# Two places in a queue: GpSimd's word ahead of a fold, and an addition moved across a block boundary

## The chip, the cores and the metric

The kernel runs on one core of a Trainium2 chip. The metric is the device time of one execution in microseconds; the median of three runs stands for the kernel. The engines have short names in the profile: PE is TensorE (matrix products; PEld its weight loads), DVE is VectorE, ACT is ScalarE, POOL is GpSimd, SP is SyncE, which only issues DMAs. Each engine takes its own instructions strictly in the order in which the program lists them; engines wait for each other through semaphores.

## The reference

Two layers run one after the other on `x` of shape (16, 256, 32, 32) in float32. Each layer normalises its input in groups (`_gn`; the 16 groups are pairs of neighbouring columns of the last axis), forms q, k and v with three 256 x 256 matrices, and lets four heads of width 64 attend over all 1024 positions. The result is added to the layer's input:

```python
q = proj(Wq, bq); k = proj(Wk, bk); v = proj(Wv, bv)
sim = jnp.einsum('bhdi,bhdj->bhij', q, k)
rel = (rel_h + rel_w).reshape(heads, d, n)
qpos = jnp.einsum('hdi,bhdj->bhij', rel, q)
attn = jax.nn.softmax(sim + qpos, axis=-1)
out = jnp.einsum('bhdn,bhmn->bhdm', v, attn)
x = x + out            # once for each layer
```

## The kernel before

**Blocks.** A *unit* `u` is one image in one layer, 32 of them. A unit has two pairs of heads (`pr`), and each pair two halves of 512 query positions (`half`). Such a half is a *block*, numbered `n` from 0 to 127; `b` = `n` mod 4 is its place in the unit, so `half` is 0 in even blocks and 1 in odd ones. `block(n)` (L619) lists the work of a block for all engines. The order is written by hand, and nothing reorders it.

**One block.** The 1024 key positions are cut into eight tiles `j`. For each, VectorE writes the position terms into a PSUM tile (`seed`, L344, product on L349), TensorE adds the product of k and q (`scores`, L373, product on L385), and ScalarE writes the exponential to a tile `p` (L394). TensorE then multiplies v with the eight tiles `p` (`attend`, L409, product on L419). Scores 0 of the next block are put between the two halves of `attend`; scores 1 to 3 come at the beginning of the block, the others further on, and between them stand two *pieces* of later work: projections to q, k or v (`project`, `values`) or the position terms (`positions`, L314). `prepare` (L593) names the pieces: in b = 1 they are a k projection and positions, in b = 3 a v projection and positions. The sums over a group for the normalisation of later units (`norm_sums`, `norm_squares`, `norm_mean`, `norm_var`) and the normalisation itself (`norm_apply`) lie on ScalarE, with two small products on TensorE and `rstd` on GpSimd (L237).

**The word.** A piece or an `attend` is done in two stretches, which write the same PSUM banks from different rows of TensorE. The second stretch may only start when the first has ended. `stretches` (L157) sees to it through GpSimd: `word` (L164) is a one-element memset (`token`, L166) on GpSimd that waits for the last product of the first stretch, and the second stretch waits for the memset. So a word stands in GpSimd's queue and goes out only after all that stands before it. Where `word` isn't called, the second stretch calls it itself.

**The denominators.** The softmax needs the sum over all keys. `add_up(blk, j)` (L397, instructions on L403 and L405) lets VectorE add tile `p` number `j` into `acc`. Additions 1 to 4 stand inside the block, addition 5 near its end, addition 6 at the beginning of the next block. Everything further is done by DMAs that accumulate, which GpSimd issues: `add_last` (L435) adds the eighth tile, `fold` (L438) adds rows 64 to 127 of `acc` to rows 0 to 63. From there on SP copies 32 rows to a *stack* that gathers the two blocks of a pair (`stack_up`, L449), GpSimd adds the other 32 rows to it (`fold_again`, L457), and `fold_stack` (L462) halves the stack's 128 rows five times (D = 64, R = 32, R/2, R/4, R/8 rows). `spread_sums` (L467) takes the four rows left to where `reciprocals` (L508) reads them in an even block; `finish` (L541) multiplies and adds the residual in an odd block.

**GpSimd's queue in an odd block** is, in order: fold D of the pair before, `add_last` of the block before, the first piece's word, fold R, `fold`, fold R/2, the `attend` word, fold R/4, `fold_again` (two DMAs), fold R/8, and in b = 3 the two instructions for `rstd`. In an even block it is: `add_last`, two words, `fold`, the `attend` word, `fold_again`. **VectorE's queue at the end of an odd block** is: addition 5, `finish`, the mean or variance out of PSUM, seeds 1 to 3 of the next block, and then in the even block addition 6, seed 4, addition 1.

The last two blocks have no pieces and are written separately (`block_without_pieces`, L756).

Of the kernel before, what the change touches and what calls it, by code (L numbers as in the profile page):

```python
# [52 lines left out]
def fast_path(ctx, tc, sh, x, layers, out, W, den_all, token, good, flag):  # L53
# [27 lines left out]
    B, C, H, N, CC, NT, NH, D, GT = (  # L81
        sh.B, sh.C, sh.H, sh.N, sh.CC, sh.NT, sh.NH, sh.D, sh.GT
    )
# [313 lines left out]
    def add_up(blk, j):  # L397
        u, pr, half = blk
        if j == 0:
            return  # L400
        if j == 1:
            accs[blk] = apool.tile([P, 2, HALF], F32, tag="acc", name=f"acc_{u}_{pr}_{half}")
            nc.vector.tensor_tensor(accs[blk], probs[blk, 0], probs[blk, 1], ALU.add)  # L403
        else:
            nc.vector.tensor_tensor(accs[blk], accs[blk], probs[blk, j], ALU.add)  # L405
# [26 lines left out]
    R = P // 4  # L432
# [29 lines left out]
    def fold_stack(u, pr, rows_):  # L462

        stack = stacks[u, pr]
        nc.gpsimd.dma_start(stack[:rows_], stack[rows_ : 2 * rows_], accum_op=ALU.add)  # L465
# [116 lines left out]
    blocks = [(u, pr, half) for u in range(NU) for pr in range(CC) for half in range(NH)]  # L582
# [36 lines left out]
    def block(n):  # L619
        blk = blocks[n]  # L620
        u, b = divmod(n, BPU)
        pr_, half = blk[1:]

        stacked = blocks[n - 3][:2] if half == 1 and n > 2 else None
        summed = blocks[n - 4][:2] if half == 0 and n > 3 else None
        before = blocks[n - 5][:2] if half == 1 and n > 4 else None
        after = blocks[n + 1] if n + 1 < len(blocks) else None
        previous = blocks[n - 1] if n > 0 else None
        one, two = u + 1 < NU, u + 2 < NU

        pieces = u + 1 < NU or b < 2
        if u + 1 == NU and b == 1:
            widen(u, 1)
        f0, f1, f2, f3 = ring
        folded = n - 1 < FOLDED
        if not pieces:
            return block_without_pieces(n, half)

        if stacked:
            fold_stack(*stacked, D)  # L640
        if previous:
            add_up(previous, 6)
            if folded:
                add_last(previous)
            else:
                add_up(previous, 7)
        for j in range(1, 4):
            scores(blk, j)
        (first, first_out), (second, second_out) = prepare(u, b)
        first(0)  # L650
        if b == 0 and one:
            norm_apply(u + 1, range(0, 1))
        if b == 1 and two:
            norm_sums(u + 2, range(9, 11))
        seed(blk, 4, f1)
        scores(blk, 4)
        add_up(blk, 1)
        if b == 0 and one:
            norm_apply(u + 1, range(1, 5))
        if b == 1 and two:  # L660
            norm_sums(u + 2, range(11, 12))
        if b == 2 and two:
            norm_squares(u + 2, range(0, 5))
        second(0)
        if half == 1:
            second_out()
        first.word()
        if half == 0:
            second.word()
        if stacked:  # L670
            fold_stack(*stacked, R)
        if previous and folded:
            fold(previous)
        if stacked:
            fold_stack(*stacked, R // 2)
        first(1)
        first_out()
        seed(blk, 5, f0)
        scores(blk, 5)
        if previous and folded:  # L680
            stack_up(previous)
        add_up(blk, 2)
        if half == 0:
            second(1)
            second_out()
        seed(blk, 6, f1)
        scores(blk, 6)
        if half == 0:
            ring[2:] = f3, f2
        seed(blk, 7, ring[2])  # L690
        scores(blk, 7)
        add_up(blk, 3)
        add_up(blk, 4)

        if after:
            seed(after, 0, f0)
        if summed:
            reciprocals(*summed)
        if n in check:
            next(checks)  # L700
        if b == 0 and one:
            norm_apply(u + 1, range(5, 9))
        if b == 0 and two:
            norm_sums(u + 2, range(0, 2))
        if b == 1 and two:
            norm_sums(u + 2, range(12, G))
        if b == 1 and one:
            norm_apply(u + 1, range(9, 11))
        if b == 2 and two:
            norm_squares(u + 2, range(5, 11))  # L710
        po = psum2(ring[3], f"po_{n}")
        values_of_p = attend(blk, po)
        values_of_p(0)
        if two and half == 1:
            if b == 1:
                mean_out = norm_mean(u + 2, filled(f1, f"pm_{n}", 0.0))
            else:
                mean_out = norm_var(u + 2, filled(f1, f"pm_{n}", EPS / 2))
        if after:
            scores(after, 0)  # L720
        values_of_p.word()
        if stacked:
            fold_stack(*stacked, R // 4)
        if previous and folded:
            fold_again(previous)
        if stacked:
            fold_stack(*stacked, R // 8)
            spread_sums(*stacked)
        if half == 1 and u + 3 < NU and units[u + 3][1] == 0 and u > 0 or n == 3:
            load_x(units[u + 3][0], range(pr_, pr_ + 1) if u > 0 else range(CC))  # L730
        add_up(blk, 5)
        if before:
            finish(*before)
        if two and half == 1:
            mean_out()
        if after:
            for j in range(1, 4):
                seed(after, j, ring[j % 3])
        if b == 0 and two:
            norm_sums(u + 2, range(2, 9))  # L740
        if b == 1 and one:
            norm_apply(u + 1, range(11, G))
        if b == 2 and two:
            norm_squares(u + 2, range(11, G))
        values_of_p(1)
        take_out(blk, po)
        pos[n] = po
# [8 lines left out]
    def block_without_pieces(n, half):  # L756

        blk = blocks[n]
        u, pr, _ = blk
        f0, f1, f2, f3 = ring  # L760
        summed = blocks[n - 2][:2] if half == 0 else (u, pr)
        before = blocks[n - 4][:2] if half == 0 else blocks[n - 3][:2]
        first = index[summed + (0,)]
        if half == 0:
            add_up(blocks[n - 1], 6)
        add_up(blocks[n - 1], 7)
        for j in range(1, 4):
            scores(blk, j)
        sums_of_p(blocks[first:n], pos[n - 1])
        keep_sums(pos[n - 1], first, n - first)  # L770
        if half == 1:
            finish(*before)
        else:
            reciprocals(*before)
        add_up(blk, 1)
        seed(blk, 7, f2)
        add_up(blk, 2)
        add_up(blk, 3)
        for j, tag in ((4, f1), (5, f0), (6, f1)):
            scores(blk, j, tag)  # L780
        reciprocals(*summed, n - first)
        scores(blk, 7)
        add_up(blk, 4)
        if half == 0:
            seed(blocks[n + 1], 0, f0)
        po = pos[n] = psum2(f3, f"po_{n}")
        values_of_p = attend(blk, po)
        values_of_p(0)
        if half == 0:
            finish(*before)  # L790
            scores(blocks[n + 1], 0)
        if half == 0:
            seed(blocks[n + 1], 1, f1)
            seed(blocks[n + 1], 2, f2)
        add_up(blk, 5)
        if half == 0:
            seed(blocks[n + 1], 3, f0)
        add_up(blk, 6)
        if half == 0:
            values_of_p(1)  # L800
            take_out(blk, po)
            return
        add_up(blk, 7)
        acc = accs.pop(blk)
        pd = psum2(f0, "pd")
        sums_on_rows(acc, pd)
        values_of_p(1)
        finish_half(u, pr, 0, outs[u, pr][:, 0, :], rdens[u, pr][:, :HALF])
        rden = rdens[u, pr][:, HALF:]
        nc.vector.reciprocal(rden, pd[:, 0, :])  # L810
        pd = psum2(f2, "pd_columns")[:, 0, : 2 * HALF // P]
        sums_on_columns(acc, pd)
        finish_half(u, pr, 1, po[:, :, :QUART], rden)
        list(in_range(flatden[:, 8 * checked : 8 * n], 1))
        list(in_range(pd, 2))
        nc.vector.tensor_reduce(good[:, 3:4], good[:, 0:3], AX.X, ALU.min)
        pc = psum2(f1, "pc")[0:1, 0, 0:1]
        nc.tensor.matmul(pc, good[:, 3:4], W.ones[:, 0:1], start=True, stop=True)
        nc.vector.tensor_copy(flag, pc)
# [404 lines left out]
```

## Time and profile before

| what | value |
|---|---|
| median of three runs | 2554.23 us (2549.47 to 2559.25) |
| the profiled execution | 2554.61 us |
| its span | 2552.8 us |
| granted TensorE clock, mean over the span | 0.998 |
| `token` memsets (L166) | 320 |
| folds of the stack (L465) | 310, 62 of each size |
| additions after the first of a block (L405) | 644, 1214 ns each |

A row of the list of waits gives the engine, what it was about to do, what ended its waiting, then the total in us, the number of times and the longest. A row of the timeline gives the start, the duration in us, the engine, the line and the tiles (what is written, an arrow, what is read), the number of instructions drawn together, and in brackets the idle time before with what ended it. The end of a matmul is modelled and reaches past the start of the next group; the step from one group to the next is therefore read from starts. A row of the DMA issues gives the queue, the count, the size and the median time from issue to landing.

### The profile page before, as it was taken

Reading aid. Unit: us, or ns where it says so; the run is one execution under the profiler, and the core shown is the slowest. Engines: PE = TensorE matmul, PEld = TensorE weight load, DVE = VectorE, ACT = ScalarE, POOL = GpSimd, SP = SyncE. Lnnn points to the kernel's source line nnn. Section 1 sums busy time; section 2 is a strip of 40 time slices with the busy share of each in tenths; the row PEclk is TensorE's granted clock in tenths of the full one; section 3 lists DMA queues with packets and bytes.
Section 4 is the critical chain, followed back from the end, with each engine's and each line's share of the span. In section 5 each row is a group of like instructions: output and inputs, shape, how many; then the busy total and the mean of one; then the engine's idle time right before and its main releaser. Section 6 shows DMA issues by size and latency. Waiting matters only on the chain.

```text
span 2552.8 us, 86089 instructions
## 1 busy us (share of the span) xinstructions
PE 2520.5 (99%) x37474; PEld 1330.9 (52%) x37474; DVE 2263.9 (89%) x2135; ACT 1950.1 (76%) x3874; POOL 836.6 (33%) x1194
## 2 busy tenths in 40 slices
PE   8999999999999999999999999999999999999997
PEld 4555555554555555555555555555555555555554
DVE  6888989988989899898899898988988999989997
ACT  6778777787777877777877778777778777787753
POOL 1333333323333233333333332333323333323320
PEclk9999999999999999999999999999999999999999
DMA  3343444454444444444444444444444444344441
GB/s 90 71 79 74 82 90 77 79 107 95 86 91 95 95 82 81 97 86 89 97 88 87 91 90 83 84 95 98 86 95 99 87 79 91 70 83 79 87 92 58
DMA packets 119537, 221.05 MB, mean 87 GB/s; under 512 B 53736, under 2 KB 55272, under 8 KB 119152
## 3 DMA queue, kind: packets, MB, share of 16 engines
q0 software_dynamic: 53568, 129.58, 30.5%
q1 hardware_dynamic: 65584, 85.90, 12.1%
q8 instruction: 295, 4.83, 0.8%
q14 instruction: 90, 0.74, 0.1%
HBM read 51.78 MB, written 17.30 MB: 27 GB/s over the span
## 4 chain that ended last, share of the span: by engine, by line
PE 88%; DMA 3%; DVE 2%; POOL 1%; issue 1%; SPq 0%; ACT 0%; POOLq 0%; DVEq 0%; ACTq 0%
PE po L419 31%; PE ps L385 31%; PE pk L268 8%; PE pv L298 8%; PE pq L268 8%; PE pa L326 2%; DMA acc<-p 1%; DMA stack<-acc 1%; DVE acc L405 1%; DVE ps L349 1%; POOL rstd L237 1%; DMA acc<-acc 0%; POOL stack L460 0%; POOL stack L465 0%; POOL acc L436 0%
## 5 line engine op out<-in xcount | busy, mean ns | idle before, releaser
L349 DVE TENSOR_TENSOR ps<-abt 128x1024 f32<-128x1024 f32 x1018 | 1227.4, 1229 | 255.2 <-ACT p L394 155.1
L394 ACT ACTIVATE p<-ps,shift 128x1024 f32<-128x1024 f32 x1024 | 1092.5, 1115 | 328.7 <-PE ps L385 325.7
L385 PE MATMUL ps<-q,k 64*64 64x512 f32 x8192 | 990.2, 591 | 0.9 <-DVE ps L349 0.9
L419 PE MATMUL po<-p,v 64*64 64x256 f32 x16384 | 930.5, 376 | 0.0
L419 PEld LDWEIGHTS po<-p,v 64*64 64x64 f32 x16384 | 628.7, 133 | 364.7 <-issue 77.7
L405 DVE TENSOR_TENSOR acc<-acc,p 128x1024 f32<-128x1024 f32 x644 | 781.6, 1214 | 4.9
L385 PEld LDWEIGHTS ps<-q,k 64*64 64x64 f32 x8192 | 303.3, 133 | 406.5 <-issue 222.8
L465 POOL DMA_DIRECT2D stack<-stack x310 | 266.7, 860 | 372.8 <-DMA stack<-acc 155.3
L166 POOL MEMSET token<- 1x1 f32 x320 | 44.8, 140 | 853.9 <-PE po L419 426.9
L268 PE MATMUL pk<-xn,Wk 64*64 64x512 f32 x2048 | 244.4, 593 | 7.0 <-POOL token L166 7.0
L460 POOL DMA_DIRECT2D stack<-acc x248 | 218.5, 1057 | 83.2 <-DMA stack<-acc 49.0
L298 PE MATMUL pv<-Wv,xn 64*64 64x256 f32 x4096 | 244.3, 376 | 0.7 <-POOL token L166 0.4
L268 PE MATMUL pq<-xn,Wq 64*64 64x512 f32 x2048 | 244.3, 592 | 0.3 <-DVE xn L910 0.3
L248 ACT ACTIVATE xn<-x,nshift,rstd 128x128 f32<-128x128 f32 x496 | 211.1, 500 | 13.7 <-POOL nshift L239 13.7
L298 PEld LDWEIGHTS pv<-Wv,xn 64*64 64x64 f32 x4096 | 153.4, 133 | 102.8 <-issue 44.2
L441 POOL DMA_DIRECT2D acc<-acc x124 | 102.4, 825 | 289.1 <-DMA acc<-p 277.8
L190 ACT ACTIVATE junk<-x,neg 128x128 f32<-128x128 f32 x498 | 195.2, 400 | 0.0
L480 ACT COPY od<-po 128x512 f32<-128x512 f32 x127 | 74.5, 586 | 115.4 <-PE po L419 115.4
L436 POOL DMA_DIRECT2D acc<-p x124 | 132.8, 1071 | 84.2 <-ACT p L394 68.4
L403 DVE TENSOR_TENSOR acc<-p,p 128x1024 f32<-128x1024 f32 x128 | 156.2, 1220 | 0.0
L268 PEld LDWEIGHTS pq<-xn,Wq 64*64 64x64 f32 x2048 | 78.6, 134 | 142.1 <-issue 129.9
L190 ACT ACTIVATE junk<-x 128x128 f32<-128x128 f32 x480 | 145.6, 314 | 0.0
(74 smaller groups left out, 1119.0 us busy)
## 6 DMA issues: line engine op xcount, KB each, us to landing
acc<-p POOLq DMA_DIRECT2D x124, 512.0 KB, 5.2
rden<-rd SPq DMA_DIRECT2D x126, 256.0 KB, 4.1
acc<-acc POOLq DMA_DIRECT2D x124, 256.0 KB, 3.5
x<-in_x_dram SPq DMA_DIRECT2D x32, 512.0 KB, 4.7
stack<-acc SPq DMA_DIRECT2D x248, 64.0 KB, 2.1
stack<-acc POOLq DMA_DIRECT2D x248, 64.0 KB, 3.3
out_dram<-x SPq DMA_DIRECT2D x31, 512.0 KB, 4.6
stack<-stack POOLq DMA_DIRECT2D x62, 128.0 KB, 2.7
```

Source lines behind the costliest of these rows:

```text
L190: nc.scalar.activation(junk, grouped(xt[units[u][0]], g), func, accum_out=into[:, g : g + 1], **bias)
L248: nc.scalar.activation(grouped(xns[u], g), grouped(xt[units[u][0]], g), AF.Identity, bias=shift[:, g : g + 1], scale=rstd[:, g : g + 1],)
L268: yield nc.tensor.matmul(pk[c, nh, :], w[l][rs, cc, c0 : c0 + D], xns[u][rs, cc, nh * HALF : (nh + 1) * HALF], start=(t == 0 and cc == 0), ...
L298: yield nc.tensor.matmul(pv[c, a, i, :], xns[u][rs, cc, j0 : j0 + D], W.wv[l][rs, cc, :], start=(t == 0 and cc == 0 and i == 0), stop=(t = ...
L349: nc.vector.tensor_tensor(ps.rearrange("p h (w y) -> p h w y", y=H), ab[:, :, :H].unsqueeze(2).to_broadcast([P, 2, XH, H]), ab[:, :, H + h ...
L385: nc.tensor.matmul(ps[c, h, :], a[hs, j0 : j0 + D], b[hs, columns], start=bool(tag) and i == 0, stop=i == len(terms) - 1, skip_group_check ...
L394: nc.scalar.activation(p, ps, AF.Exp, bias=W.shift)
L403: nc.vector.tensor_tensor(accs[blk], probs[blk, 0], probs[blk, 1], ALU.add)
L405: nc.vector.tensor_tensor(accs[blk], accs[blk], probs[blk, j], ALU.add)
L419: yield nc.tensor.matmul(po[c, a, :QUART], vts[u][rs, j, c0 : c0 + D], p[rs, h, a * QUART : (a + 1) * QUART], start=(t == 0 and j == 0), s ...
L460: nc.gpsimd.dma_start(at, acc[R:D, h, :], accum_op=ALU.add)
L465: nc.gpsimd.dma_start(stack[:rows_], stack[rows_ : 2 * rows_], accum_op=ALU.add)
```

## The change

In odd blocks fold D moves from the beginning of the block to behind the first piece's word, and fold R to behind `fold`; folds R/2, R/4 and R/8 keep their places. GpSimd's queue becomes: `add_last`, the word, fold D, `fold`, fold R, fold R/2, the `attend` word and so on. Addition 5 of an odd block moves from the end of that block, ahead of `finish`, to the beginning of the next block, ahead of addition 6. In even blocks it stays. The number of instructions and DMAs is the same.

```diff
@@ block(n)
-        if stacked:
-            fold_stack(*stacked, D)
         if previous:
+            if half == 0:
+                add_up(previous, 5)
             add_up(previous, 6)
             if folded:
                 add_last(previous)
...
         if half == 0:
             second.word()
         if stacked:
-            fold_stack(*stacked, R)
+            fold_stack(*stacked, D)
         if previous and folded:
             fold(previous)
         if stacked:
+            fold_stack(*stacked, R)
             fold_stack(*stacked, R // 2)
...
-        add_up(blk, 5)
+        if half == 0:
+            add_up(blk, 5)
         if before:
             finish(*before)
@@ block_without_pieces(n, half)
         if half == 0:
+            add_up(blocks[n - 1], 5)
             add_up(blocks[n - 1], 6)
         add_up(blocks[n - 1], 7)
```

## The prediction

> **What bounds the kernel now.** I read the page's shares first, then its chain.
>
> ```profile
> PE 2520.5 (99%) x37474; PEld 1330.9 (52%) x37474; DVE 2263.9 (89%) x2135; ACT 1950.1 (76%) x3874; POOL 836.6 (33%) x1194
> ...
> PE 88%; DMA 3%; DVE 2%; POOL 1%; issue 1%; SPq 0%; ACT 0%; POOLq 0%; DVEq 0%; ACTq 0%
> ```
>
> TensorE sets the end. No matmul is removed, so the gain can only be time in which TensorE stands still. Then the list of waits:
>
> ```profile
> POOL stack L465 <- DMA stack<-acc: 155.3, 49, 5.2
> ...
> PEld po L419 <- POOL token L166: 38.5, 127, 0.6
> ...
> PE pk L268 <- POOL token L166: 7.0, 4, 2.7
> ```
>
> The last row: TensorE waited four times, 7.0 us, for GpSimd's word before the second stretch of a k projection. The middle row (the word inside `attend`) is 0.3 us a time at a weight load, with the matmuls before it still running: free. The first row is GpSimd held 155.3 us at folds of the stack. The timeline of one late block (block 29) joins the rows; TensorE, then GpSimd:
>
> ```profile
> 608.83 1.11 PE L326 MATMUL pa<-rel,q 64*64 64x64 f32 x64
> 611.75 1.95 PE L268 MATMUL pk<-xn,Wk 64*64 64x512 f32 x16 [1.81 <-POOL token L166]
> ```
> ```profile
> 603.84 1.69 POOL L460 DMA_DIRECT2D stack<-acc  x2 [3.74 <-DMA stack<-acc]
> 609.89 0.84 POOL L465 DMA_DIRECT2D stack<-stack  x1 [4.37 <-DMA stack<-acc]
> 610.43 1.23 POOL L436 DMA_DIRECT2D acc<-p  x1
> 611.01 0.69 POOL L166 MEMSET token<- 1x1 f32 x1
> ```
>
> The first fold (609.89) waits until the stack's DMAs have landed; `add_last` and the word queue behind it, the word is out at 611.70, TensorE goes on at 611.75. The positions take 0.93 in a block that doesn't wait, so the next group was due at 609.76: 1.99 lost (the 1.81 counts from a modelled end).
>
> I took such differences of starts over all 128 blocks, each group against the usual step of its kind. Late words in b = 1 blocks: 2.85, 1.99, 1.45, 1.44, 0.20 and 0.14, together **8.1**. The longest has a sequel, in the table of windows:
>
> ```profile
> 136.30:140.10 3.80, 1.16 (x68) 0.97 (x60) 3.80 (x4) 2.31 (x4) 1.79 (x3) 1.00 0.23 43
> 140.10:144.20 4.10, 4.08 (x24) 1.43 (x28) 2.61 (x3) 0.75 (x1) 0.80 (x1) 0.58 0.89 158
> ```
>
> Second figure PE busy, third from last the granted clock: after the stall it was 0.58, and the next groups took 1.32 and 0.43 too long, **1.8**. The third kind is small and regular:
>
> ```profile
> 997.54 2.75 PE L385 MATMUL ps<-q,k 64*64 64x512 f32 x24
> ...
> 1015.80 2.83 PE L385 MATMUL ps<-q,k 64*64 64x512 f32 x24
> 1018.45 1.90 PE L268 MATMUL pq<-xn,Wq 64*64 64x512 f32 x16
> ```
> ```profile
> 1013.98 3.50 DVE L349 TENSOR_TENSOR ps<-abt 128x1024 f32<-128x1024 f32 x3
> 1017.39 1.22 DVE L405 TENSOR_TENSOR acc<-acc,p 128x1024 f32<-128x1024 f32 x1
> 1018.52 1.23 DVE L349 TENSOR_TENSOR ps<-abt 128x1024 f32<-128x1024 f32 x1
> ```
>
> Scores 1 to 3 took 2.83 at the start of an even block, 2.75 at that of an odd one. VectorE's third seed ends at 13.98 + 3.50 = 1017.48, and the third group of scores would begin at 15.80 + 2 x 0.86 = 1017.52, too close for the wait between engines. 52 of 62 even blocks lose 0.08: **4.2**. The rest of what TensorE loses lies at the program's ends, in two late words of even blocks (0.37 and 0.40) and in 0.03 after each small mean, none of it touched.
>
> **The word ahead of the fold.** Nothing is added or removed, the order of GpSimd's queue changes. `add_last` needs addition 6 of the block before; in block 49 that ends at 997.84, and in almost every odd block at the same place. In the even block above it ends at 1018.61 and `add_last` starts at 1019.18, 0.57 later; so here it goes out at 998.4 (now 1002.11, behind the fold), or 0.54 behind the last `fold_again` where that is later: 604.9 in block 29. The word then follows the first stretch's end, 608.2 there, 1.5 before TensorE needs it. All of 8.1 + 1.8 = **9.9** goes. [...]
>
> **What the fold's later place costs.** The first fold (D) starts behind the word, and the third (R/2) must leave before the `attend` word. The rows for the path:
>
> ```profile
> acc<-p POOLq DMA_DIRECT2D x124, 512.0 KB, 5.2
> ...
> acc<-acc POOLq DMA_DIRECT2D x124, 256.0 KB, 3.5
> ...
> stack<-stack POOLq DMA_DIRECT2D x62, 128.0 KB, 2.7
> ```
>
> In block 49: `add_last` 998.4, landing 5.2 to 6.8 (its own landing now) later, 1003.6 to 1005.2; word 1002.3, D 1002.7. By 2.7 alone D lands at 1005.4. [...] The trace agrees: in all 61 odd blocks the fold issued behind `add_last` landed after it, by 0.7 to 2.6. So D lands at 1005.4 to 1006.4; `fold` leaves 0.3 after `add_last` landed, 1003.9 to 1005.5, landing by 1009.0; R leaves at 1005.7 to 1006.7 and lands behind `fold`, 1008.3 to 1009.4; R/2 leaves by 1009.7. The `attend` word may be out by 1012.3, when the second half of `attend` starts, so R/2 may leave until 1011.6: at least 1.9 to spare. By the 2.7 alone, without the queue, it would be 1008.4. In block 29: D still 609.9, R about 614, R/2 616 to 618.5, and the limit without the stall is 617.8: up to 0.7 is lost. The same for the other late blocks gives 1.4 in the one at 136 us, 0.1 in that at 845, nothing elsewhere. Bounds: 0, and the 8.1 if each late block loses at the second word what it gains at the first; I take **2.2**.
>
> Behind R/2 stand R/4, `fold_again`, R/8 and, in b = 3 blocks, `rstd` with the next block's `add_last` and word. R/4 is held by the `attend` word anyway, so R/8 moves only where R/2 lands over 3 us after leaving, and an even block's word is late only when R/8 is over 1.6 late. SP's `stack_up` waits for `fold`, now earlier; its `spread_sums` for R/8, with some 10 us until VectorE reads the sums. 0 to 1; I take 0.
>
> **The fifth addition.** One VectorE instruction of 1.22 (1.13 from start to start) per odd block goes from ahead of `finish` to ahead of addition 6. VectorE has no idle time between the two places (no brackets in the rows), so `finish`, the mean and seeds 1 to 3 start 1.13 earlier. Seed 3 needs the exponential of scores 0, done at 1013.71; it would start at 1015.1 and end at 1016.4. The 4.2 goes (bounds 0 and 4.2). Addition 6, `add_last` and seed 4 behind it stay where they are. That is the cover: seed 4 ends at 1019.75 and is read at 1020.16, and if seeds 1 to 3 could not use the freed time, seed 4 would be up to 0.7 late, 62 x 0.7 = 43.
>
> **Sum.** 9.9 + 4.2 - 2.2 = 11.9. The profiled execution took 2554.61 (span 2552.8), 0.4 from the median 2554.23; 2554.6 - 11.9 = **2542.7**.
>
> **Rivals.**
> 1. *The wait moves*: the late blocks pay at the `attend` word what they saved, because D can't start before the stack has landed in either order. For it: D unchanged in block 29. Against: `add_last` and `fold`, which R/2 stood behind, leave 5 and 2 earlier there. Only 4.2 and perhaps the clock's 1.8 remain: 2554.6 - 5 = 2549.6.
> 2. *The seeds don't help*: another wait stands just behind seed 3. Then 9.9 - 2.2: 2546.9.
> 3. *Slower*: place, the `attend` word of every odd block; mechanism, three folds in series behind a 512 KB DMA. Folds now took up to 5.0 from issue to landing behind `add_last`; if D and R both took 4.7, D would land at 1007.4, R leave at 1007.7 and land at 1012.4, and R/2 leave at 1012.7, 1.1 past the limit: 61 x 1.1 = 67, 2554.6 + 67 - 14 = 2608. It decides when the mean loss is 14 / 61 = 0.23. Against it: `add_last` leaves early, so that its bytes are mostly gone when D comes.
>
> **How the numbers follow.** My forecast 0.66, rival 1 0.14, rival 2 0.11, rival 3 0.09. A measurement here can tell about 0.5%, 12.8 us: below 2541.5 is faster, above 2567 slower. My case alone spans 2540.6 (no new waits) to 2547. The range takes in rivals 1 and 2: 2540 to 2553. Faster: about half of my case, 0.34; slower: most of rival 3, 0.07; same 0.59.
>
> **What would show it.** Right: no wait of pk for the token in b = 1; scores 1 to 3 of even blocks at 2.75; no stretch of half clock inside; `add_last` of odd blocks starting some 3.7 earlier. Wrong: TensorE waiting for the token before `po`, or seeds of even blocks waiting for ACT.

## The result

| | median of the runs | ratio to the kernel before, 95% interval |
|---|---|---|
| before | 2557.65 us (2549.47 to 2563.05, 8 runs) | |
| after | 2544.82 us (2543.09 to 2550.51, 8 runs) | 0.9961 (0.995 to 0.9971) |

By the ratio, the change makes the kernel faster by 0.39% (0.29 to 0.5%): about 10 us, where 11.9 were forecast. The time forecast was 2542.7. The two medians of the table lie 12.8 apart, at the far end of that interval; the median of before is higher than the one shown to the prediction because five more runs came in. The profiled execution of after took 2544.62, 10.0 less than that of before, with a span of 2542.9 in place of 2552.8.

### The profile after

The page's shares and its chain, as for before:

```profile
PE 2514.2 (99%) x37474; PEld 1335.6 (53%) x37474; DVE 2269.4 (89%) x2135; ACT 1949.5 (77%) x3874; POOL 835.1 (33%) x1194
...
PE 94%; DVE 2%; POOL 1%; issue 1%; DMA 1%; SPq 0%; ACT 0%; POOLq 0%; DVEq 0%; ACTq 0%
```

The counts are the same, and the chain holds 94% TensorE in place of 88%. DMA has 1% of it in place of 3%: in before, much of that 3% lay ahead of three of the late words (those at about 608, 845 and 1705 us). A share of the chain is not a loss: 6% of the span would be 150 us, and the spans differ by 9.9. The list of waits (engine, what it was about to do, what ended it; total, times, longest):

```profile
POOL stack L465 <- DMA stack<-stack: 277.6, 164, 4.0
...
POOL stack L465 <- DMA stack<-acc: 7.0, 5, 2.7
...
PE po L419 <- POOL token L166: 2.1, 2, 1.2
...
PE pv L298 <- POOL token L166: 1.4, 4, 0.3
```

The row of pk waiting for the token, 7.0 before, does not appear. GpSimd's waiting at the folds for the stack's DMAs fell from 155.3 to 7.0. Its waiting has for the most part moved, not gone: at the folds it now waits 277.6 for the fold before, 99.2 before, but behind the first word. Two rows are new or larger: `po` waits for the token twice, which is the second half of `attend`, and pv four times (twice before), which is the first word of a unit. The timeline of block 29, GpSimd and then TensorE:

```profile
601.82 1.69 POOL L460 DMA_DIRECT2D stack<-acc  x2 [4.07 <-DMA stack<-acc]
602.94 1.49 POOL L436 DMA_DIRECT2D acc<-p  x1
605.98 0.09 POOL L166 MEMSET token<- 1x1 f32 x1 [1.55 <-PE pk L268]
607.24 0.83 POOL L465 DMA_DIRECT2D stack<-stack  x1 [1.18 <-DMA stack<-acc]
```
```profile
606.49 1.11 PE L326 MATMUL pa<-rel,q 64*64 64x64 f32 x64
607.42 1.90 PE L268 MATMUL pk<-xn,Wk 64*64 64x512 f32 x16
```

The fold still waits for the stack (607.24), but nothing that TensorE needs stands behind it. The word went out at 605.98, and pk follows the positions after 0.93. The stretch of half clock is gone too: in before the granted clock was 0.50 for 3.41 us, from 140.59 to 144.00, and in after it is 1.00 there. The table of windows has, second from the left PE busy and third from the right the granted clock:

```profile
136.30:140.10 3.80, 3.80 (x96) 2.00 (x92) 3.80 (x4) 3.13 (x5) 0.83 (x1) 1.00 0.87 169
140.10:144.20 4.10, 4.10 (x65) 2.29 (x60) 4.07 (x6) 4.10 (x11) 1.61 (x2) 1.00 0.53 88
```

The start of the even block after block 49, TensorE and VectorE:

```profile
1009.50 2.75 PE L385 MATMUL ps<-q,k 64*64 64x512 f32 x24
```
```profile
1006.55 3.50 DVE L349 TENSOR_TENSOR ps<-abt 128x1024 f32<-128x1024 f32 x3
1009.96 2.48 DVE L405 TENSOR_TENSOR acc<-acc,p 128x1024 f32<-128x1024 f32 x2
1012.36 1.23 DVE L349 TENSOR_TENSOR ps<-abt 128x1024 f32<-128x1024 f32 x1
```

Scores 1 to 3 take 2.75, not 2.83. Seed 3 ends at 1010.05, 1.2 before the third group of scores begins (1009.50 + 2 x 0.86 = 1011.22). Additions 5 and 6 now stand together, and seed 4 follows as close as before. No even block loses time there any more.

Losses of TensorE by steps from start to start, added over all blocks, in the two profiled executions:

| place | before | after |
|---|---|---|
| word ahead of pk, b = 1 | 8.1 | 0.0 |
| half clock after the longest of these | 1.8 | 0.0 |
| scores 1 to 3 of even blocks | 4.2 | 0.0 |
| `attend` word, odd blocks | 0.0 | 2.5 |
| first word of a unit, b = 0 | 0.8 | 2.1 |

The column's sums differ by 14.9 - 4.6 = 10.3; the spans differ by 9.9.

### The profile page after: what moved, and what is told of

Same layout as the page of the kernel before. It is cut to its first block, busy times and chain, and to the rows that moved or that the text cites. A ratio compares the mean times of both kernels' runs of the same rounds, so it can differ in the third digit from the quotient of the medians.

```text
span 2542.9 us, 86134 instructions
## 1 busy us (share of the span) xinstructions
PE 2514.2 (99%) x37474; PEld 1335.6 (53%) x37474; DVE 2269.4 (89%) x2135; ACT 1949.5 (77%) x3874; POOL 835.1 (33%) x1194
## 4 chain that ended last, share of the span: by engine, by line
PE 94%; DVE 2%; POOL 1%; issue 1%; DMA 1%; SPq 0%; ACT 0%; POOLq 0%; DVEq 0%; ACTq 0%
PE po L419 33%; PE ps L385 33%; PE pv L298 8%; PE pk L268 8%; PE pq L268 8%; PE pa L326 2%; DVE acc L405 1%; DVE ps L349 1%; POOL rstd L237 1%; DMA stack<-stack 0%; POOL stack L465 0%; POOL stack L460 0%; PE pm L209 0%; DMA x<-in_x_dram 0%; DMA rden<-rd 0%
## 5 line engine op out<-in xcount | busy, mean ns | idle before, releaser
L385 PEld LDWEIGHTS ps<-q,k 64*64 64x64 f32 x8192 | 308.5, 133 | 395.7 <-issue 275.1
L465 POOL DMA_DIRECT2D stack<-stack x310 | 249.6, 805 | 338.7 <-DMA stack<-stack 277.6
L166 POOL MEMSET token<- 1x1 f32 x320 | 35.8, 112 | 830.4 <-PE po L419 400.7
L436 POOL DMA_DIRECT2D acc<-p x124 | 115.5, 931 | 227.8 <-ACT od L480 128.5
L441 POOL DMA_DIRECT2D acc<-acc x124 | 109.5, 883 | 206.0 <-DMA acc<-p 197.0
```

The costliest lines, as they stand in the source:

```text
L385: nc.tensor.matmul(ps[c, h, :], a[hs, j0 : j0 + D], b[hs, columns], start=bool(tag) and i == 0, stop=i == len(terms) - 1, skip_group_check ...
```

## The experiments

All times are medians; each ratio is to runs of the kernel before that were made beside it on the same chip. `word_only`, `add_only`, `fold_between` and `fold_late` ran beside a before of 2557.39.

### Each part alone

`word_only` has only the order of the folds changed:

```diff
-        if stacked:
-            fold_stack(*stacked, D)
         if previous:
             add_up(previous, 6)
...
         if stacked:
-            fold_stack(*stacked, R)
+            fold_stack(*stacked, D)
         if previous and folded:
             fold(previous)
         if stacked:
+            fold_stack(*stacked, R)
             fold_stack(*stacked, R // 2)
```

> Only the folds are moved behind the word; addition 5 of odd blocks stays at the end of its block. The theory that the two parts add up: late words of b = 1 blocks give 8.1 and the half clock 1.8, some 2.5 come back at attend words, so about 7 us under the kernel before; scores 1 to 3 of even blocks still take 2.83, the pk products wait for no token. The rival that the addition made the whole gain: no change against before, and the profile still shows pk waiting for the token.

Measured: 2550.99, ratio 0.9977 (0.9965 to 0.9989), that is 3 to 9 us under before. From its list of waits:

```profile
PE pv L298 <- POOL token L166: 2.9, 3, 1.3
...
PE po L419 <- POOL token L166: 2.6, 2, 1.7
```

No row of pk, as expected; scores 1 to 3 lose 4.0 in total, much as before (4.2). The late words at `attend` (3.0 together) and at the start of units (3.4) are there without the moved addition, so they belong to the folds' new order or were there before it. They explain why less came of it than the 7 expected: 9.9, less 3.0, less the 2.6 by which the words of units cost more than in before, is 4.3, and the profiled span is 4.0 shorter.

`add_only` has only the addition moved:

```diff
         if previous:
+            if half == 0:
+                add_up(previous, 5)
             add_up(previous, 6)
...
-        add_up(blk, 5)
+        if half == 0:
+            add_up(blk, 5)
```

> Only addition 5 of odd blocks is moved; the folds stand as before. The theory: scores 1 to 3 of even blocks fall from 2.83 to 2.75, 52 x 0.08 = 4.2 us under the kernel before, and the late words of b = 1 blocks (a varying 5 to 15 us) stay. The rival that seed 3 is not what held them: no change, still 2.83. A second rival, that seed 4 comes late: scores 4 of even blocks wait and the time rises.

Measured: 2553.74, ratio 0.9986 (0.9976 to 0.9996), 1 to 6 us under before. The waits and one start of an even block:

```profile
PE pk L268 <- POOL token L166: 7.8, 5, 2.6
```
```profile
1015.03 2.75 PE L385 MATMUL ps<-q,k 64*64 64x512 f32 x24
```

The seeds' loss is gone in all 62 even blocks, the late words stay. Seed 4 held nothing up. The two parts alone give 0.23% and 0.14%; together 0.39 to 0.44% was measured (three times, below). The sum of the parts, 0.37%, lies within those intervals, and each part leaves the other's wait as it was: as far as these runs can tell, they add up.

### What held the word: the fold's wait, or the queue's length

`fold_between` leaves fold D ahead of the word, but puts it behind `add_last`. Fold R goes behind `fold`, as in the changed kernel. The addition is not moved.

```diff
-        if stacked:
-            fold_stack(*stacked, D)
         if previous:
             add_up(previous, 6)
             if folded:
                 add_last(previous)
             else:
                 add_up(previous, 7)
+        if stacked:
+            fold_stack(*stacked, D)
...
-        if stacked:
-            fold_stack(*stacked, R)
         if previous and folded:
             fold(previous)
         if stacked:
+            fold_stack(*stacked, R)
             fold_stack(*stacked, R // 2)
```

> Fold D stands behind add_last but still ahead of the word; addition 5 as before. The theory that the word was held by the fold's wait for the stack's DMAs: late words remain, each about 0.55 shorter (add_last's issue no longer lies behind the wait), so 2 to 4 us under the kernel before, with pk still waiting for the token in the late blocks. The rival that the length of the queue ahead of the word, add_last above all, was what counted: as fast as with the folds behind the word, about 7 us under.

Measured: 2549.45, ratio 0.997 (0.9958 to 0.9982). By the median this is more than the theory's 2 to 4, and what the rival forecast. The profile shows the theory's mechanism; the waits, then GpSimd in block 29:

```profile
PE pk L268 <- POOL token L166: 4.1, 3, 2.2
```
```profile
604.95 1.49 POOL L436 DMA_DIRECT2D acc<-p  x1
609.51 0.83 POOL L465 DMA_DIRECT2D stack<-stack  x1 [3.07 <-PE pa L326]
610.05 0.32 POOL L166 MEMSET token<- 1x1 f32 x1
```

`add_last` is out at 604.95, fold D waits until the second DMA of `fold_again` has landed in the stack (609.22 by the record; the product named in the bracket isn't its input), and the word goes out only behind it. It still waits for the fold at the same blocks: 2.38, 1.13 and 1.12 are lost at 136, 608 and 844 us, where it was 2.85, 1.99 and 1.45; behind the first, the next groups still take 1.06 and 0.69 too long (1.32 and 0.43 in before). The fourth loss, at about 1700 us, is gone. So the late words became shorter by 0.33 to 0.86, where 0.55 was reckoned for `add_last`'s place. In all, the profiled span is 2549.9, 2.9 under before, as the theory had it. That execution was the slowest of ten, and what the other runs gained beyond it no profile shows: the mechanism is the theory's, but the time doesn't decide against the rival. No `attend` word is late in this order, while `word_only` pays 3.0 there. The two orders' intervals overlap, and these runs don't tell which of them is better.

`between_add` is this order with the addition moved as in the changed kernel; it ran later, beside a before of 2558.17 and the changed kernel again.

> The changed kernel once more, as the measure for the next two on the same chip: some 11 us under the kernel before.

> The order add_last, fold D, word, now with addition 5 of odd blocks moved as in the changed kernel. The theory that the addition's part is independent of the folds' place: 4 us under the same order without it (2549.5), that is 2545 to 2546, level with the changed kernel; a few late words of pk stay and no attend word is late. The rival that add_last's earlier issue was the main part of the gain: clearly under the changed kernel.

Measured: the changed kernel 2547.08, ratio 0.9956 (0.994 to 0.9973); `between_add` 2546.69, ratio 0.9958 (0.9944 to 0.9973). They are level. Its profile still has late words of pk (4.0 in all) and no late `attend` word. Fold D behind the word is thus one of two ways to the same time: what one order loses at pk, the other loses at `attend` and at the first words of units (3.1 and 3.8 in this profile of the changed kernel, 0.0 and 1.6 in that of `between_add`). Both have `add_last` ahead of fold D and fold R behind `fold`; neither was run alone.

### The margin at the `attend` word

`fold_late` moves fold D one place further, behind `fold`:

```diff
-        if stacked:
-            fold_stack(*stacked, D)
         if previous and folded:
             fold(previous)
         if stacked:
+            fold_stack(*stacked, D)
             fold_stack(*stacked, R)
             fold_stack(*stacked, R // 2)
```

> As the changed kernel, but fold D one place later still, behind fold. The theory, with the margin of some 2 to 3 us at the attend word that the prediction worked out: D now stands behind the 256 KB of fold in the DMA queue, lands some 3 later, R/2 leaves at about 1012 where 1011.6 is the limit in block 49, and most odd blocks lose 0.3 to 1 us at the attend word: 20 to 55 us over the changed kernel. The rival that the margin is ample: within 3 us of the changed kernel.

Measured: 2611.96, ratio 1.0217 (1.0195 to 1.0239), 67 over the changed kernel's 2544.82; somewhat beyond the 20 to 55 expected. This is the prediction's third rival brought about. One odd block, TensorE and then GpSimd, and the waits:

```profile
1422.82 1.07 PE L385 MATMUL ps<-q,k 64*64 64x512 f32 x8
1424.64 3.68 PE L419 MATMUL po<-p,v 64*64 64x256 f32 x64 [0.75 <-POOL token L166]
```
```profile
1415.75 0.83 POOL L441 DMA_DIRECT2D acc<-acc  x1 [2.13 <-DMA acc<-p]
1416.55 0.87 POOL L465 DMA_DIRECT2D stack<-stack  x1
1420.86 0.78 POOL L465 DMA_DIRECT2D stack<-stack  x1 [3.44 <-DMA stack<-stack]
1423.78 0.77 POOL L465 DMA_DIRECT2D stack<-stack  x1 [2.14 <-DMA stack<-stack]
1424.28 0.30 POOL L166 MEMSET token<- 1x1 f32 x1
```
```profile
PE po L419 <- POOL token L166: 39.8, 33, 4.7
```

Fold D goes out right behind `fold`, R 4.3 later, R/2 another 2.9 later, and the `attend` word comes only then, at 1424.28. Over the 61 odd blocks the median of D's landing is 4.04 after its issue, and 2.92 in the changed kernel; R/2 leaves 9.7 after the first word, and 7.05 in the changed kernel. With the prediction's numbers for block 49 the limit is 9.3 after the word. So the changed kernel has about 2.3 to spare in the median, and an order that differs by one place has none. By steps from start to start the profile loses 45 us at the `attend` words of 38 odd blocks, which is in the range expected. Behind the four longest of these the next group took 1.5 to 1.7 too long, 6.7 together, and the first words of units lose 7.8: these two the expectation had left out.

### Trying to win back the new losses

`rstd_first` puts fold R/8, `spread_sums` and the load of x behind the mean and `rstd`; `half_later` also sends R/2 out behind the `attend` word and R/4 with R/8. They ran beside a before of 2554.74 and the changed kernel again.

`rstd_first`:

```diff
         if previous and folded:
             fold_again(previous)
-        if stacked:
-            fold_stack(*stacked, R // 8)
-            spread_sums(*stacked)
...
         if two and half == 1:
             mean_out()
+        if stacked:
+            fold_stack(*stacked, R // 8)
+            spread_sums(*stacked)
```

`half_later`, against `rstd_first`:

```diff
             fold_stack(*stacked, R)
-            fold_stack(*stacked, R // 2)
...
         values_of_p.word()
         if stacked:
-            fold_stack(*stacked, R // 4)
+            fold_stack(*stacked, R // 2)
...
         if stacked:
+            fold_stack(*stacked, R // 4)
             fold_stack(*stacked, R // 8)
```

> The changed kernel itself, as the measure for the next two on the same chip: some 12 us under the kernel before.

> As the changed kernel, but fold R/8 (with spread_sums and the load of x behind it) stands behind the mean and rstd on GpSimd. The theory that the late words at the start of a unit (four of 0.53 in the changed kernel) come from rstd waiting behind R/8: rstd starts as soon as its variance is there, some 2 us earlier, these words are in time, and ScalarE's 18 us of waiting for nshift goes; 1 to 2 us under the changed kernel. The rival that R/8 isn't what delays rstd: the same words stay late and the time is the same.

> As the one before, and fold R/2 moves behind the attend word, R/4 to R/8 behind rstd. The theory: no attend word can be late for a fold any more, so the two losses of 1.1 and 1.4 us go: 3 to 4 us under the changed kernel. The rival: the last folds come late, so that add_last and the words of the next even block, or VectorE's reciprocals, wait for them: no gain, or up to 10 us over the changed kernel.

Measured: the changed kernel 2545.04, ratio 0.9958 (0.9942 to 0.9975). `rstd_first` 2545.23, ratio 0.9957 (0.9941 to 0.9973), no gain. ScalarE's waiting for `nshift` fell from 16.0 to 6.7, as the theory said, and three late words at the start of a unit cost only 0.27 each. A fourth costs 2.6, and the next group 1.6 more: there `fold_again` was late (its second DMA, after 2.29 of the standing still that is described below, under the loss at 457 us), and R/8 now stands between `rstd` and `add_last`.

`half_later` took 2565.42, ratio 1.0042 (1.0026 to 1.0057), 20 over the changed kernel; the rival was right. Its waits, and the queue at the start of a unit:

```profile
PE pv L298 <- POOL token L166: 17.2, 30, 2.8
```
```profile
978.29 0.78 POOL L239 TENSOR_TENSOR nshift<-neg,rstd 128x16 f32<-128x16 f32 x1
979.03 0.87 POOL L465 DMA_DIRECT2D stack<-stack  x1
981.63 0.81 POOL L465 DMA_DIRECT2D stack<-stack  x1 [1.73 <-DMA stack<-stack]
982.15 1.23 POOL L436 DMA_DIRECT2D acc<-p  x1
982.72 0.83 POOL L166 MEMSET token<- 1x1 f32 x2
```

R/8 waits 1.73 for R/4 to land, `add_last` stands behind it, and the first word is late by some 0.57 in most of the 30 units that wait. It is the fault of the kernel before over again, at another place: a DMA that waits for a landing, in front of a word.

`both_words` therefore treats the two kinds of odd block differently. In b = 1, R/2 goes behind the `attend` word and R/4 behind `fold_again`; in b = 3 the mean and `rstd` go ahead of `fold_again` and R/8. `rest_of_sums` is a new function that holds `fold_again`, in b = 1 R/4, then R/8, `spread_sums` and the load of x.

```diff
         if stacked:
             fold_stack(*stacked, R)
-            fold_stack(*stacked, R // 2)
+            if b == 3:
+                fold_stack(*stacked, R // 2)
...
-            fold_stack(*stacked, R // 4)
+            fold_stack(*stacked, R // 4 if b == 3 else R // 2)
+        if b != 3:
+            rest_of_sums()
...
         if two and half == 1:
             mean_out()
+        if b == 3:
+            rest_of_sums()
```

> As the changed kernel, but in b = 1 fold R/2 goes out behind the attend word and R/4 behind fold_again; in b = 3 the mean and rstd go ahead of fold_again and R/8. The theory: the late attend words lie in b = 1 alone, where no rstd and no early add_last stand behind the folds, so the 2.5 us go; in b = 3 rstd waits neither for R/8 nor for a late fold_again, so the late words at the start of a unit, about 2 us, go too: 3 to 4 us under the changed kernel. The rival, as where R/2 was moved in all blocks: add_last of the next even block stands behind the late folds, and the time is level or up to 10 us over.

Measured beside the changed kernel's 2547.08: 2545.52, ratio 0.9954 (0.9938 to 0.9971). No late `attend` word is left. Two late words at the start of units remain, 0.9 and 2.6. `add_last` stands behind `fold_again` there, and `fold_again` was late; GpSimd at the second:

```profile
1907.90 1.77 POOL L460 DMA_DIRECT2D stack<-acc  x2 [2.77 <-issue]
```

It did not wait for `stack_up`, which SP had issued at 1895.27: the profile names no releaser here, nor for the 2.47 at the first. What this is, is told below, under the loss at 457 us. The difference of 1.6 us to the changed kernel lies inside both intervals. Nothing that was tried is measurably faster than the changed kernel.

## Why the prediction was right

**What bounds the kernel.** Right. All that was gained is TensorE's standing time; its instruction counts are the same.

**The word ahead of the fold.** Right in place and size: 9.9 in the profile, clock included. In block 29 the word was forecast for 608.2 by the clock of before; it came at 605.98, where the block's positions begin 2.34 earlier than before (606.49, not 608.83), so 608.3. That the half clock went with the stall fits its being the stall's sequel. Two runs that keep a stall at that place have slow groups behind it and support it: `add_only` (2.80, then 1.54 too long) and `fold_between` (2.38, then 1.06 and 0.69). In the profile of before, the granted clock stayed at 1.00 behind the stalls of 1.4 to 2.0. What lowers the clock, no run shows.

**What the later fold costs.** 2.2 was forecast, at 136 us (1.4), 604 (0.7) and 845 (0.1); 2.5 was measured, at 145 us (1.1), 457 (1.35) and 849 (0.1). The first and last are the blocks named; the one at 604 lost nothing. So the blocks named cost 1.2, not 2.2, and that the sum still came out is chance. The prediction had counted TensorE waiting ahead of `po` among the signs of being wrong; it did wait, at this small price. Block 49 can be followed in GpSimd's queue, 6.3 earlier throughout than in the profile of before:

```profile
992.12 0.88 POOL L436 DMA_DIRECT2D acc<-p  x1 [1.57 <-ACT od L480]
995.88 0.09 POOL L166 MEMSET token<- 1x1 f32 x1 [2.88 <-PE pk L268]
996.50 0.83 POOL L465 DMA_DIRECT2D stack<-stack  x1 [0.53 <-issue]
997.46 0.81 POOL L441 DMA_DIRECT2D acc<-acc  x1
1001.17 0.78 POOL L465 DMA_DIRECT2D stack<-stack  x1 [2.90 <-DMA stack<-stack]
1003.91 0.77 POOL L465 DMA_DIRECT2D stack<-stack  x1 [1.95 <-DMA stack<-stack]
1005.41 0.09 POOL L166 MEMSET token<- 1x1 f32 x1 [0.73 <-PE pm L209]
```

With 6.3 added: `add_last` 998.4 (forecast 998.4), D 1002.8 (1002.7), `fold` 1003.8 (1003.9 to 1005.5), R 1007.5 (1005.7 to 1006.7), R/2 1010.2 (by 1009.7), the limit 1011.6. D landed 4.4 after its issue here, at 1007.2, where 1006.4 was the latest forecast (2.92 is the median). So R and R/2 were 0.8 and 0.5 later than forecast, and 1.4 of the 1.9 to spare was left. It was right to let D and R land behind what was issued ahead of them: in the profiles of before and of after, none of GpSimd's 806 DMAs landed earlier than one issued ahead of it. By the 2.7 alone R/2 was due at 1008.4. One figure of that step was wrong: the folds behind `add_last` landed 0.16 to 3.3 after it in the profile of before, not 0.7 to 2.6; the order held in all 61.

The loss at 457 us was not foreseen:

```profile
449.49 1.12 POOL L441 DMA_DIRECT2D acc<-acc  x1
456.29 0.78 POOL L465 DMA_DIRECT2D stack<-stack  x1 [5.68 <-issue]
459.00 0.77 POOL L465 DMA_DIRECT2D stack<-stack  x1 [1.93 <-PE ps L385]
```

R left 3.5 after D had landed by the record (452.80), and the profile names nothing that it waited for. This R is the 129th DMA that GpSimd issues, and the standing still goes with the count. In all twelve profiles GpSimd is idle for 2.3 to 6.5 us, with no releaser named, ahead of its 129th, 250th, 371st, 492nd, 613th and 734th DMA, 121 apart, whichever DMA stands there: 5.34, 2.29, 3.37, 3.31, 2.73 and 5.23 us in before, 5.68, 2.30, 3.37, 2.57, 2.74 and 5.34 in after. In the kernel before, the 129th is `fold`, idle for 5.34 ahead of it and at no cost. In the changed kernel no other of GpSimd's 806 DMAs has over 2 us of such idle time ahead of it. Here the 129th is a fold ahead of the `attend` word, which it cost 1.7 to 2.1 in both repeats of the changed kernel, in `word_only` and in `rstd_first`. The 250th and the 613th stand a little ahead of the first words of the units at about 820 and 1910 us, and these two are late in every profile. Why GpSimd stands still at these DMAs no run shows.

**The words behind the chain.** 0 was taken out of 0 to 1; it was 1.3 (four late words of 0.53 in place of two of 0.4). This is the step that was too low. `word_only` has 3.4 there, and `add_only`, with the old order of folds, 2.7, so it varies from one execution to the next, and only part of it can be laid to the change. Two of the four, like both of before, follow the 250th and the 613th DMA.

**The fifth addition.** Right: 4.2 forecast and 4.2 gone in the profile; 1 to 6 us by the runs of `add_only`.

**The sum.** With these sizes it is 9.9 + 4.2 - 2.5 - 1.3 = 10.3, where 11.9 was forecast.

**The rivals.** The waits moved only in part (2.5 of 8.1), and the seeds did help. The slower rival has the right mechanism, as `fold_late` shows. That its price fits too (2608 reckoned, 2612 measured) is in part chance: it was reckoned for the `attend` word alone, which took 45 us in the profile of `fold_late`. It stayed away from the changed kernel for the reason that the prediction gave: `add_last` goes out early, and D landed 2.92 after its issue in the median, not 4.7.

## What to carry to other kernels

In block 29 of before, GpSimd stood idle for 4.37 us until the stack's DMAs had landed and fold D could go out; `add_last` and the word came behind it, and TensorE lost 1.99. So in GpSimd's queue an instruction that another engine is waiting for belongs ahead of a DMA that has to wait for another's landing, and so does a long DMA that the rest of the chain needs (by before's clock, `add_last` of block 49 went out at 998.4 in place of 1002.11). Before moving such a wait, count the landings that come in series between its new place and the next instruction that somebody waits for: here two landings, of D and of R, fit with about 2.3 us to spare, and one place further cost 67 us. The addition that was moved on busy VectorE cost nothing: VectorE had no idle time between its two places, and what had stood behind it started earlier by its length (by 1.13 in block 50, seeds 1 to 3 at 1012.85 by before's clock, not 1013.98).

## What was not expected of the hardware

For these folds, what stood in front of one in the queue mattered more than its size. Fold R, 64 KB, took 3.5 us in the median from issue to landing in before and 2.5 in after. In the changed kernel the folds of 8 to 64 KB took 2.17 to 2.47 us in the median, and that of 128 KB 2.92, behind a nearly finished `add_last` (in block 49 `add_last` landed 0.68 after D's issue); right behind `fold`'s 256 KB, in `fold_late`, it took 4.04. Behind the stall of 2.85 us in before, at 136 us, TensorE's granted clock was 0.50 for 3.41 us, and the next groups took 1.32 and 0.43 too long; behind one of 2.4 in `fold_between`, at 139 us, the next two groups took 1.06 and 0.69 too long; behind one of 3.0 in `half_later`, at 822 us, none did. In these profiles the length of the stall alone doesn't decide.
